# Graph layers on one core: the steps of tile 0's values and of the destination blocks set apart, and the hand-over from layer 0 to layer 1 ordered anew

## Chip, core and metric

One core of a Trainium2 chip runs the whole kernel. The metric is the device time of one execution in microseconds (us). The engines are called as in the profile: PE (TensorE), DVE (VectorE), ACT (ScalarE), POOL (GpSimd) and SP, which here only issues DMAs. Each engine works through its own instructions in the order in which the program gives them; an instruction whose input is late holds all that stand behind it.

## Reference, cut to what matters

Four graph layers run one after the other on 2708 nodes with 128 features. The change lies at the end of layer 0 and the start of layer 1.

```python
h = jnp.maximum(_layernorm(x), 0.0)
x = x + (adj.T @ h) / adj.sum(axis=0)[:, None]            # layer 0
h = jnp.maximum(_layernorm(x), 0.0)
s = h @ msg_w[:, :D].T                                     # layer 1: "sources", of row i
d = h @ msg_w[:, D:].T                                     # "destinations", of column j
messages = gelu(s[:, None, :] + d[None, :, :] + msg_b)     # only where adj is not zero
aggregated = einsum('ijd,ij->id', messages, adj)
new = gelu(concat([h, aggregated]) @ upd_w.T + upd_b) + h
x = x + layernorm(new)
# layer 2: a GRU over adj @ h;  layer 3: two heads of masked attention
```

About 0.6% of `adj` is not zero. Layer 1 is therefore done on lists of the non-zero entries.

## The kernel before

**Tiles and sets.** The nodes are cut into 22 tiles of 128 rows (the last has 20) and six groups of four tiles (the last, `LAST` = 5, has two).

**Layer 0** walks over `adj` in cuts `(c, s)`: columns of group `c`, rows of group `s`. This text calls the six cuts of one `c` a round and one cut a set. In each set DVE lists the eight largest entries of every row in each block (`list_cut`: MAX8 and FIND_INDEX8, lines 352 and 354), PE transposes the cut and multiplies it with `h0` (`work_cut`, lines 399 and 384), ACT copies the transposes out (line 406), and a DMA writes them to `adjT`. The columns of group 5 have no round of their own: their cuts (`z`) are worked in the sets of round 4 that `PARTS` names. Steps of the rows whose sums are ready are put between: norms of a finished group, its rows turned (`turn_rows`, lines 150 and 152), and its destinations.

**Three parts of a number.** Layer 1 gathers with bf16 matmuls of ones and zeros, so each f32 operand is kept as three bf16 parts. The lead is an ACT copy, the rest is src minus lead on DVE, the second part is an ACT copy of the rest, and the third part is rest minus second part on POOL. For the destinations of a group these are lines 240, 247, 248 and 249, with the scratch tile `d_rest`; for the values of a tile lines 554 to 557 (`split`) or 560 and 563 to 565 (`lead_of`, `rest_of`). A value tile also gets its columns and row ends from two POOL copies (`describe_columns`, lines 572 and 573). It all lands in `xb[t % 2]`, three parts, columns and ends side by side.

**One tile of layer 1.** `spread_ends` and `select_rows` (DVE 550 and 586) compare row numbers with the list ends and give `sel`; two DMAs move it by one row into `later`; `finish_rows` (DVE 604) subtracts. `fetch` (PE 618, ACT 619 and 623) gathers values and columns into list order through `sel`; `place` (DVE 631 to 652) picks `value` and `where`; `pass_on` (PE 668, ACT 670, one DMA) and `spread_columns` (one DMA) hand the column numbers to all partitions; `columns` (DVE 914) makes the second matrix of ones, `cols`. `find_rows` (DVE 586, tile `mine`), `put_values` (eight POOL instructions, line 897) and `put_more` (ACT 906) build the weighted matrices `put`.

**Period t of layer 1** works on four tiles at once, in six steps k. `combine(t, k)` adds sources and destinations of four blocks in PSUM (lines 971 and 975), `activate` is the Gelu (ACT 983), `gather` multiplies with `put` (PE 996). Meanwhile tile t+1 is put, tile t+2 is fetched and placed, and the rows of tile t+3 are selected.

**The start of layer 1** does not fit this pattern, since nothing has been begun. A list `run(...)` after layer 0 and a table `opening`, one row for each k of period 0, hold what has to be made up for: groups 4 and 5 are normed, turned and made into destinations here, and tiles 0 and 1 are brought forward. `manual_schedule` keeps the order of the program on every engine. PSUM tiles that are named through `bank` share two slots, so the third such tile waits until one of the two before it has been read.

Of the kernel before, what the change touches and what calls it, by code (L numbers as in the profile page):

```python
# [30 lines left out]
P = 128  # L31
N = 2708
D = 128
# [18 lines left out]
def size(t):  # L52
    return min(P, N - t * P)
# [7 lines left out]
def listed_layers(ctx: ExitStack, tc: tile.TileContext, x, adj, w, out, flag):  # L61
# [177 lines left out]
        for src, dst, q0, q1, k in state["d", g]:  # L239
            nc.scalar.copy(dst[0], src)  # L240

    def split_destinations(g):

        rest = d_rest
        for src, dst, q0, q1, k in state.pop(("d", g)):
            r = rest[0:k, q0:q1, :]
            nc.vector.tensor_tensor(r, src, dst[0], ALU.subtract)
            nc.scalar.copy(dst[1], r)
            nc.gpsimd.tensor_tensor(dst[2], r, dst[1], ALU.subtract)  # L249

# [276 lines left out]

    def last_destinations():
        destinations(LAST - 2)
        yield  # L530

    def list_last(n):
# [39 lines left out]
        nc.gpsimd.tensor_copy(x[:, :, 3 * S : 4 * S], col[:, t, :, :])  # L572
        nc.gpsimd.tensor_copy(x[:, :, C - 1], ends[:, t, :])

    def rest_tile(t):
        r = d_rest[:, 2 * t : 2 * t + 2, :].rearrange("p q d -> p (q d)")
        return r[:, 0 : NB * S].rearrange("p (b s) -> p b s", s=S)

    def describe(t, rest):
        split(*values_of(t), rest)  # L580
# [93 lines left out]
    def spread_columns(t):  # L674
# [4 lines left out]
            st["spread"].rearrange("p b e -> p (b e)"), st.pop("passed").rearrange("b e -> (b e)").partition_broadcast(P)  # L679
        )  # L680

    PARTS = {1: (0,), 2: (1, 2), 3: (3,), 4: (4, 5)}
    order = [(c, s) for c in range(LAST) for s in range(len(GROUPS))]
    mask_near(0, 0)
    for i, (c, s) in enumerate(order):
        g0, gk = GROUPS[s]
        list_cut(c, s, g0)
        if i == 0:
            state["f", 0] = factors(*state.pop(("m", -1)))
            list_cut(c, s, g0 + 1)  # L690
            state["m", 1] = moments(tiles_of(xs, *GROUPS[1]), "n4")
            list_cut(c, s, g0 + 2)
            state["f", 1] = factors(*state.pop(("m", 1)))
            list_cut(c, s, g0 + 3)
# [12 lines left out]
        if i + 1 < len(order):  # L707
            mask_near(*order[i + 1])
        if i > BEHIND and i - 1 - BEHIND + RING < len(order):
            load_cut(*order[i - 1 - BEHIND + RING])  # L710
        for z in {(LAST - 2, 3): (0,), (LAST - 2, 4): (1,), (LAST - 2, 5): (2,), (LAST - 1, 2): (3,), (LAST - 1, 3): (4, 5)}.get(
            (c, s), ()
        ):
            load_cut(LAST, z)
        if c > 0 and s == (2 if c < LAST - 1 else 1):
            turn_sums(c - 1)
        if (c, s) == (LAST - 1, LAST):
            turn_rows(LAST - 2)
            turn_sums(LAST)
        work_cut(c, s, first_steps(s) if c == 0 else next_steps(c, s))  # L720
        if c > 1 and s == 0:
            turn_rows(c - 2)
        if c > 1 and s == 1:
            destinations(c - 2)
        if c > 1 and s == (3 if c < LAST - 1 else 2):
            split_destinations(c - 2)
        if c == LAST - 1:
            if s == 1:
                ranked = rank(0, FIRST, bank("p_r"))
            if s == LAST - 1:  # L730
                pass_on(0)
            for z in PARTS.get(s, ()):
                mask_near(LAST, z)
                work_cut(LAST, z)
            if s == 1:
                nc.vector.tensor_copy(*ranked)
                spread_ends(0)
                select_rows(0)
            if s == 2:
                describe(0, rest_tile(0))  # L740
                finish_rows(0)
            if s == 3:
                for q in range(2):
                    fetch(0, q)
                place(0)
            if s == LAST - 1:
                for _ in lift(LAST):
                    pass

        if (c, s) == (1, 2):  # L750
            nc.sync.dma_start(msg_wT, w["msg_wT"])
        if (c, s) == (2, 3):
            nc.sync.dma_start(msg_b, w["msg_b"].partition_broadcast(P))
            nc.gpsimd.tensor_copy(src_self[:, 0, :], msg_wT[:, 0, :])
            nc.gpsimd.tensor_tensor(src_self[:, 1, :], msg_wT[:, 0, :], msg_wT[:, 1, :], ALU.add)

    write_one()

    add(LAST)
    measure(LAST)  # L760
    for _ in lift(LAST - 1):
        pass
    split_destinations(LAST - 2)
    turn_sums(LAST - 1)
    ending.close()
    l0.close()
# [32 lines left out]
    with (  # L799
# [116 lines left out]
        own_rows, aggs, projected = {}, {}, {}  # L916

        def project(k):

            p = projected[k] = bank("p_s") if k else mpool.tile([P, 4, D], F32, name="p_m").rearrange("p q d -> p (q d)")  # L920
            for q in range(2):
                c, mq = (2 * k + q) * P, size(2 * k + q)
                nc.tensor.matmul(
                    p[0:mq, q * 2 * D : (q + 1) * 2 * D], hT[:, c : c + mq],
                    src_self.rearrange("p c d -> p (c d)"), start=True, stop=True,
                )

        def sources(k):

            if k not in projected:  # L930
                project(k)
            pv = projected.pop(k).rearrange("p (t c d) -> p t c d", t=2, c=2)
            sb = once.tile([P, 2, 2, D], F32, name="sb")
            m = size(2 * k + 1)
            if m < P:
                nc.vector.memset(sb[:, 1, :, :], 0.0)
            bv = msg_b.unsqueeze(1).to_broadcast([P, 2, D])
            if m == P:
                bv = msg_b.unsqueeze(1).unsqueeze(1).to_broadcast([P, 2, 2, D])
                nc.vector.tensor_tensor(sb, pv, bv, ALU.add)  # L940
            else:
                for q in range(2):
                    mq = size(2 * k + q)
                    nc.vector.tensor_tensor(sb[0:mq, q, :, :], pv[0:mq, q, :, :], bv[0:mq, :, :], ALU.add)
            s3 = three.tile([P, 3, 2, D], BF16, name="s3")
            lead_of([s3[:, q, :, :] for q in range(3)], sb[:, :, 0, :])
            state["sb"] = sb
            own_rows[k] = s3, None

        def sources_rest(k):  # L950
# [135 lines left out]
        def period(t, opening):  # L1086
# [6 lines left out]
            for k in range(GB):  # L1093
# [22 lines left out]
                        project(t // 2 + 1)  # L1116
                if (t, k) in mixes:
                    mix(mixes[t, k])
                if k in ((1, 2) if begun else (4, 5)) and b:
                    fetch(t + 2, k - (1 if begun else 4))  # L1120
                if k == 1 and a:
                    lead_of(*values_of(t + 3))
                if k == 1:
# [14 lines left out]
                    check_lists()  # L1138
                if k > 0 and c and begun:
                    put_more(t + 1, k)  # L1140
                if k > 2 and not begun:
                    for q in range(2 * k - 6 + (k == 3), min(2 * k - 4, GB)):
                        put_more(t + 1, q)
                if k == (3 if begun else GB - 1) and c:
                    columns(t + 1)
                if k == 3 and t == WIDE_AT:
                    place_wide()
                if k == (3 if begun else GB - 1) and b:
                    place(t + 2)
# [27 lines left out]
        def run(*steps):  # L1177
            for step, *numbers in steps:
                step(*numbers)

        run(
            (spread_columns, 0), (spread_ends, 1), (select_rows, 1), (sources, 0), (find_rows, 0), (describe, 1, rest_tile(1)),
            (rows, 5), (sources_rest, 0), (add, 4), (measure, 4), (put_values, 0), (turn_rows, 5), (columns, 0),
            (put_more, 0, 1), (put_more, 0, 2), (finish_rows, 1),
        )
        opening = {
            0: ((put_more, 0, 3),),
            1: ((fetch_both, 1), (spread_ends, 2), (select_rows, 2), (rows, 4)),
            2: ((put_more, 0, 4), (place, 1), (find_rows, 1), (turn_rows, 4), (put_more, 0, 5)),
            3: ((describe_next, 2), (finish_rows, 2), (pass_on, 1), (spread_columns, 1), (destinations, 4), (put_values, 1)),  # L1190
            4: ((split_destinations, 4), (destinations, 5)),
            5: ((split_destinations, 5),),
        }
        for t in range(NT + 1):
            period(t, opening if t == 0 else {})
# [878 lines left out]
```

## Time and profile before

| | |
|---|---|
| median of 3 runs | 998.86 us (998.2 to 1002.5) |
| the profiled execution | 1005.51 us, of which its span is 1003.7 us |
| busy in the span | PE 918.7, DVE 793.0, ACT 532.0, POOL 444.0 us |
| mean granted TensorE clock | 0.955 |

Times inside the execution are counted from the start of its span. Layer 0 ends, and layer 1 begins, at about 200 us. A view of windows gives for each stretch the busy time of PE, of PE's weight loads, of DVE, ACT and POOL, then the granted clock and the load of the DMA engines. In a view of waits, "A <- B: total, times, longest" says that engine A sat idle until B had finished. In a timeline each row is start, duration, engine, line and operation; brackets hold the idle time before it and what ended it.

### The profile page before, as it was taken

What the parts mean: (1) busy time and instruction counts of PE and PEld (TensorE: products, weight loads), DVE (VectorE), ACT (ScalarE), POOL (GpSimd) and SP (SyncE); (2) the same over time, 40 slices, a digit from 0 to 9 for tenths busy, and PEclk for the clock granted to TensorE, in tenths of its full rate; (3) what the DMA queues carried; (4) which work ended last, traced back from release to release, by engine and by line L of the source; (5) the groups of instructions that cost most, each with busy time, mean ns of one, the idle gap of its engine ahead of it and who ended that gap; (6) DMA issues with size and microseconds to landing.
All of it is one profiled execution on the core that took longest, in us unless ns stands there. A gap on an engine that the chain in (4) does not pass through costs nothing. (4 is left out here: it accounts for less than half of the span.)

```text
span 1003.7 us, 21971 instructions
## 1 busy us (share of the span) xinstructions
PE 918.7 (92%) x7948; PEld 746.5 (74%) x7948; DVE 793.0 (79%) x2753; ACT 532.0 (53%) x1561; POOL 444.0 (44%) x524
## 2 busy tenths in 40 slices
PE   6799998964999999999999999999889999999983
PEld 3465555663999999899899644444678999999972
DVE  8999998772988898979965565666488977997793
ACT  5776665663665767656666324332321653564342
POOL 5402221354987596967975444444111300430142
PEclk9999999865999999999999899999899999999996
DMA  9899997422544443334323365764301674457000
GB/s 336 276 353 359 351 364 265 164 64 77 164 134 134 127 146 109 112 101 133 105 89 122 119 201 190 242 207 151 92 22 56 192 238 135 149 184 221 6 17 15
DMA packets 81736, 163.61 MB, mean 163 GB/s; under 512 B 9100, under 2 KB 27056, under 8 KB 81618
## 3 DMA queue, kind: packets, MB, share of 16 engines
q1 hardware_dynamic: 62518, 129.98, 40.5%
q10 hardware_dynamic: 19100, 32.13, 8.7%
q8 instruction: 64, 1.05, 0.4%
q14 instruction: 54, 0.44, 0.1%
HBM read 115.47 MB, written 30.87 MB: 146 GB/s over the span
## 5 line engine op out<-in xcount | busy, mean ns | idle before, releaser
L897 POOL TENSOR_SCALAR put<-count,line,value 128x128 f32<-128x128 f32 x176 | 195.3, 1122 | 18.7 <-DVE value L652 18.0
L1283 PE MATMUL att<-hv,wt 128*128 128x129 f32 x1672 | 196.2, 278 | 7.4 <-DVE wt L1253 6.0
L1283 PEld LDWEIGHTS att<-hv,wt 128*128 128x128 f32 x1672 | 192.5, 194 | 10.5 <-DVE wt L1253 8.5
L975 PE MATMUL p_m<-d,cols 128*128 128x128 bf16 (+1 forms) x1452 | 163.9, 222 | 16.8 <-POOL d L249 9.1
L971 PE MATMUL p_m<-s,sel 128*128 128x128 bf16 x1452 | 163.5, 222 | 6.6 <-ACT g L983 6.2
L1253 DVE SCALAR_TENSOR_TENSOR wt<-row,lift,mask 128x1024 f32<-128x1024 f32 (+1 forms) x132 | 138.8, 1082 | 23.3 <-PE att L1283 23.2
L121 POOL TENSOR_TENSOR n_r<-n_r,minus_half 128x4 f32<-128x4 f32 (+1 forms) x28 | 40.4, 1441 | 243.3 <-DVE n_r L120 241.6
L996 PE MATMUL agg<-put,g 128*128 128x128 f32 (+1 forms) x968 | 128.0, 286 | 0.0
L996 PEld LDWEIGHTS agg<-put,g 128*128 128x128 f32 x968 | 117.3, 198 | 2.5 <-issue 0.4
L384 PE MATMUL sums<-a,h 128*128 128x512 f32 x220 | 116.7, 627 | 1.6 <-ACT h L137 1.6
L971 PEld LDWEIGHTS <-sel 128*128 128x128 bf16 x1452 | 104.5, 99 | 17.1 <-issue 16.5
L983 ACT ACTIVATE g<-p_m 128x512 f32<-128x512 f32 x132 | 72.8, 553 | 76.0 <-PE agg L996 48.3
L975 PEld LDWEIGHTS <-cols 128*128 128x128 bf16 (+1 forms) x1452 | 102.7, 99 | 11.6 <-issue 5.5
L1444 PE MATMUL p_agg<-a,hs 128*128 128x512 f32 (+2 forms) x264 | 108.1, 551 | 2.6 <-DMA a<-adjT 2.5
L399 PEld LDWEIGHTS p_T<-ident,a 128*128 128x128 f32 (+1 forms) x440 | 55.7, 145 | 63.3 <-issue 41.2
L906 ACT ACTIVATE put<-mine,value 128x128 f32<-128x128 bf16 x308 | 100.8, 393 | 0.0
L354 DVE FIND_INDEX8 col<-val,a 128x8 uint16<-128x128 f32 x327 | 89.3, 284 | 0.0
L1444 PEld LDWEIGHTS p_agg<-a,hs 128*128 128x128 f32 (+1 forms) x264 | 47.3, 192 | 50.0 <-issue 45.7
L406 ACT ACTIVATE aT<-p_T 128x512 f32<-128x512 f32 (+2 forms) x132 | 71.0, 540 | 23.6 <-PE p_T L399 21.2
L399 PE MATMUL p_T<-ident,a 128*128 128x128 f32 (+1 forms) x440 | 71.3, 283 | 12.9 <-ACT aT L406 6.7
L1406 ACT ACTIVATE hs<-hs 128x1354 f32<-128x1354 f32 (+1 forms) x44 | 58.5, 1329 | 39.8 <-DMA hs<-in_adj 39.4
L352 DVE MAX8 val<-a 128x8 f32<-128x128 f32 x327 | 77.2, 276 | 0.0
(292 smaller groups left out, 1522.5 us busy)
## 6 DMA issues: line engine op xcount, KB each, us to landing
hs<-in_adj SPq DMA_DIRECT2D x42, 677.0 KB
adjT<-aT ACTq DMA_DIRECT2D x50, 512.0 KB
a<-adjT SPq DMA_DIRECT2D x20, 1280.0 KB
a<-in_adj SPq DMA_DIRECT2D x24, 1024.0 KB
spread<-passed SPq DMA_DIRECT2D x22, 704.0 KB
later<-sel SPq DMA_DIRECT2D x22, 616.0 KB
cols_a<-in_adj SPq DMA_DIRECT2D x11, 320.0 KB
row<-own_d ACTq DMA_DIRECT2D x10, 256.0 KB
```

What stands on the lines that cost most here:

```text
L352: nc.vector.max(val[0:m, n, b, :], v)
L354: nc.vector.max_index(col[0:m, n, b, :], val[0:m, n, b, :], v)
L384: nc.tensor.matmul(accs[c][:, 0:w], h0[0:m, n, :], a[0:m, n - g0, t0 * P - lo : t0 * P - lo + w], start=(n == 0), stop=(n == NT - 1),)
L399: nc.tensor.transpose(p[0:k, i * iw + q * P : i * iw + q * P + m], a[0:m, q, e : e + k], ident[0:m, 0:m])
L897: nc.gpsimd.tensor_scalar(st["put", 0][:, b, :], count, st["line"][:, b : b + 1], st["value"][:, b : b + 1], ALU.is_equal, ALU.mult,)
L906: nc.scalar.activation(st["put", 1][:, b - HP, :], st["mine"][:, b - HP, :], AF.Identity, scale=st["value"][:, b : b + 1])
L971: nc.tensor.matmul(p[:, b - b0, :], st["sel"][:, b, :], s3[:, q, t % 2, :], start=(q == 0), stop=False)
L975: nc.tensor.matmul(p[:, b - b0, :], st["cols"][0:kb, b, :], d3[0:kb, b, q, :], start=False, stop=(q == 2))
L996: nc.tensor.matmul(agg, g[:, b - 4 * k, :], put, start=(b == 0), stop=False)
L1253: nc.vector.scalar_tensor_tensor(wt[:, 0:n], row[:, k, c : c + n], lift[:, j, k : k + 1], mask[:, j, c : c + n], op0=ALU.max, op1=ALU.mult,)
L1283: nc.tensor.matmul(banks[s // 3][:, s % 3, :], wt[:, q * P : (q + 1) * P], hv[:, j, k, :], start=(v < 2 and s // 3 not in touched), stop=( ...
L1444: nc.tensor.matmul(pa[:, 0:n], h[0:k, j, :], a[0:k, j - j0, 0:n], start=(j == 0), stop=(j == NT - 1))
```

## The change

It sets steps apart that stood together, and orders the end of layer 0 and the start of layer 1 anew.

- **Destinations in layer 0.** `split_destinations` becomes `take_lead` (the DVE subtraction, in set 2 of a round) and `split_rest` (the ACT copy and the POOL subtraction, in set 3).
- **Values of tile 0.** `describe(0)` in set 2 of round 4 becomes `lead_of` (ACT, set 1), `less_lead` (DVE, set 2) and `pass_rest` (ACT and POOL, set 3). The rest has a tile of its own instead of a part of `d_rest`.
- **Placing of tile 0.** `place(0)` moves from set 3 to set 4, and `pass_on(0)` from set 4 into set 5, where the projection for the sources of tiles 0 and 1 (`project(0)`) now follows it.
- **End of layer 0.** Tile 1's values, the bias of the sources and the last norm of group 5 come ahead of the last turned sums.
- **Run and opening.** Group 5's destinations and group 4's norm come into the run; group 4's destinations come ahead of `combine(0, 2)`; `fetch_both(2)` comes ahead of `combine(0, 4)`; the puts of tile 0 stand later, and those of tile 1 have other places.

```diff
-    def split_destinations(g):
+    def take_lead(g, rest=None):
+        state["r", g] = []
         for src, dst, q0, q1, k in state.pop(("d", g)):
-            r = rest[0:k, q0:q1, :]
+            r = (d_rest if rest is None else rest)[0:k, q0:q1, :]
             nc.vector.tensor_tensor(r, src, dst[0], ALU.subtract)
+            state["r", g].append((r, dst))
+    def split_rest(g):
+        for r, dst in state.pop(("r", g)):
             nc.scalar.copy(dst[1], r)
             nc.gpsimd.tensor_tensor(dst[2], r, dst[1], ALU.subtract)
...
     def last_destinations():
         destinations(LAST - 2)
+        pass_on(0)
+        project(0)
         yield
...
+    def less_lead(t):
+        dst, src = values_of(t)
+        rest = state["x", t] = opener.tile([P, NB, S], F32, name="hot")
+        nc.vector.tensor_tensor(rest, src, dst[0], ALU.subtract)
+    def pass_rest(t):
+        dst, rest = values_of(t)[0], state.pop(("x", t))
+        nc.scalar.copy(dst[1], rest)
+        nc.gpsimd.tensor_tensor(dst[2], rest, dst[1], ALU.subtract)
+        describe_columns(t)
...
         work_cut(c, s, first_steps(s) if c == 0 else next_steps(c, s))
+        if c > 1 and s == 3:
+            split_rest(c - 2)
+        if (c, s) == (LAST - 1, 3):
+            pass_rest(0)
...
-        if c > 1 and s == (3 if c < LAST - 1 else 2):
-            split_destinations(c - 2)
+        if c > 1 and s == 2:
+            take_lead(c - 2)
...
-            if s == LAST - 1:
-                pass_on(0)
...
                 select_rows(0)
+                lead_of(*values_of(0))
             if s == 2:
-                describe(0, rest_tile(0))
+                less_lead(0)
                 finish_rows(0)
             if s == 3:
                 for q in range(2):
                     fetch(0, q)
+            if s == LAST - 1:
                 place(0)
...
     write_one()
+    lead_of(*values_of(1))
+    take_lead(LAST - 2, pool.tile([P, 4, D], F32, bufs=1, name="part_x"))
     add(LAST)
     measure(LAST)
+    less_lead(1)
+    add_bias(0, d_rest.rearrange("p (t c) d -> p t c d", t=2))
+    spread_ends(1)
+    split_rest(LAST - 2)
+    rows(LAST)
+    pass_rest(1)
     for _ in lift(LAST - 1):
         pass
-    split_destinations(LAST - 2)
     turn_sums(LAST - 1)
...
-                if k in ((1, 2) if begun else (4, 5)) and b:
-                    fetch(t + 2, k - (1 if begun else 4))
+                if k in (1, 2) and b and begun:
+                    fetch(t + 2, k - 1)
...
-                if k > 2 and not begun:
-                    for q in range(2 * k - 6 + (k == 3), min(2 * k - 4, GB)):
+                if not begun:
+                    for q in {4: (1, 2), 5: (3, 4, 5)}.get(k, ()):
                         put_more(t + 1, q)
...
         run(
-            (spread_columns, 0), (spread_ends, 1), (select_rows, 1), (sources, 0), (find_rows, 0), (describe, 1, rest_tile(1)),
-            (rows, 5), (sources_rest, 0), (add, 4), (measure, 4), (put_values, 0), (turn_rows, 5), (columns, 0),
-            (put_more, 0, 1), (put_more, 0, 2), (finish_rows, 1),
+            (spread_columns, 0), (select_rows, 1), (take_sources, 0), (turn_rows, 5), (sources_rest, 0), (add, 4), (measure, 4),
+            (destinations, 5), (take_pair, 5), (split_rest, 5), (columns, 0), (rows, 4), (put_values, 0), (finish_rows, 1),
+            (spread_ends, 2), (find_rows, 0),
         )
         opening = {
-            0: ((put_more, 0, 3),),
-            1: ((fetch_both, 1), (spread_ends, 2), (select_rows, 2), (rows, 4)),
-            2: ((put_more, 0, 4), (place, 1), (find_rows, 1), (turn_rows, 4), (put_more, 0, 5)),
-            3: ((describe_next, 2), (finish_rows, 2), (pass_on, 1), (spread_columns, 1), (destinations, 4), (put_values, 1)),
-            4: ((split_destinations, 4), (destinations, 5)),
-            5: ((split_destinations, 5),),
+            1: ((turn_rows, 4), (fetch_both, 1), (select_rows, 2), (put_more, 0, 1)),
+            2: ((destinations, 4), (put_more, 0, 2), (put_more, 0, 3), (take_lead, 4), (place, 1)),
+            3: (
+                (split_rest, 4), (pass_on, 1), (spread_columns, 1), (describe_next, 2), (finish_rows, 2),
+                (put_more, 0, 4), (put_more, 0, 5),
+            ),
+            4: ((fetch_both, 2), (find_rows, 1), (put_values, 1)),
+            5: ((place, 2),),
         }
```

`project` and `add_bias` are the two halves of the old `sources`, brought out of layer 1's block; `take_sources` is the rest of it (the lead of the sources, on ACT). For tiles 0 and 1 the projection's PSUM tile is now one of layer 0's sums tiles, and the biased sources lie in `d_rest` instead of a tile of their own. `take_pair(5)` is `take_lead` with a scratch tile of layer 1, and `find_rows(0)` and `find_rows(1)` stand later than before. In periods after the first, the program is the same.

More of the change, by code (lines that the diff above doesn't have):

```diff
@@ L240, in destinations @@
             nc.scalar.copy(dst[0], src)
-    def split_destinations(g):
-        rest = d_rest
+    def take_lead(g, rest=None):
+        state["r", g] = []
         for src, dst, q0, q1, k in state.pop(("d", g)):
-            r = rest[0:k, q0:q1, :]
+            r = (d_rest if rest is None else rest)[0:k, q0:q1, :]
             nc.vector.tensor_tensor(r, src, dst[0], ALU.subtract)
+            state["r", g].append((r, dst))
+    def split_rest(g):
+        for r, dst in state.pop(("r", g)):
             nc.scalar.copy(dst[1], r)
@@ L573, in describe_columns @@
         nc.gpsimd.tensor_copy(x[:, :, C - 1], ends[:, t, :])
-    def rest_tile(t):
-        r = d_rest[:, 2 * t : 2 * t + 2, :].rearrange("p q d -> p (q d)")
-        return r[:, 0 : NB * S].rearrange("p (b s) -> p b s", s=S)
+    def less_lead(t):
[7 more added lines that the diff above has]
+        describe_columns(t)
     def describe(t, rest):
@@ L680, in spread_columns, with project, add_bias @@
         )
+    own_rows, projected = {}, {}
+    def project(k):
+        p = projected[k] = bank("p_s") if k else sump.tile([P, CH], F32, name="sums")
+        for q in range(2):
+            c, mq = (2 * k + q) * P, size(2 * k + q)
+            nc.tensor.matmul(
+                p[0:mq, q * 2 * D : (q + 1) * 2 * D], hT[:, c : c + mq],
+                src_self.rearrange("p c d -> p (c d)"), start=True, stop=True,
+            )
+    def add_bias(k, sb):
+        state["sb"] = sb
+        pv = projected.pop(k).rearrange("p (t c d) -> p t c d", t=2, c=2)
+        m = size(2 * k + 1)
+        if m < P:
+            nc.vector.memset(sb[:, 1, :, :], 0.0)
+            bv = msg_b.unsqueeze(1).to_broadcast([P, 2, D])
+            for q in range(2):
+                mq = size(2 * k + q)
+                nc.vector.tensor_tensor(sb[0:mq, q, :, :], pv[0:mq, q, :, :], bv[0:mq, :, :], ALU.add)
+        else:
+            bv = msg_b.unsqueeze(1).unsqueeze(1).to_broadcast([P, 2, 2, D])
+            nc.vector.tensor_tensor(sb, pv, bv, ALU.add)
     PARTS = {1: (0,), 2: (1, 2), 3: (3,), 4: (4, 5)}
@@ L744, in listed_layers @@
                     fetch(0, q)
+            if s == LAST - 1:
                 place(0)
-            if s == LAST - 1:
                 for _ in lift(LAST):
@@ L914, in columns, with take_sources @@
             nc.vector.tensor_scalar(st["cols"], st.pop("spread"), part, None, ALU.is_equal)
[L916 to L926, printed above, removed]
+        aggs = {}
         def sources(k):
+            sb = once.tile([P, 2, 2, D], F32, name="sb")
             if k not in projected:
                 project(k)
[L932 to L944, printed above, removed]
+            add_bias(k, sb)
+            take_sources(k)
+        def take_sources(k):
             s3 = three.tile([P, 3, 2, D], BF16, name="s3")
-            lead_of([s3[:, q, :, :] for q in range(3)], sb[:, :, 0, :])
-            state["sb"] = sb
+            lead_of([s3[:, q, :, :] for q in range(3)], state["sb"][:, :, 0, :])
             own_rows[k] = s3, None
@@ L1147, in period @@
                     place_wide()
+                if k == 3 and b and begun:
+                    place(t + 2)
                 if k == (3 if begun else GB - 1) and b:
-                    place(t + 2)
                     find_rows(t + 2)
@@ L1179, in run, with take_pair @@
                 step(*numbers)
-        run(
-            (spread_columns, 0), (spread_ends, 1), (select_rows, 1), (sources, 0), (find_rows, 0), (describe, 1, rest_tile(1)),
-            (rows, 5), (sources_rest, 0), (add, 4), (measure, 4), (put_values, 0), (turn_rows, 5), (columns, 0),
-            (put_more, 0, 1), (put_more, 0, 2), (finish_rows, 1),
+        def take_pair(g):
+            take_lead(g, once.tile([P, 2, D], F32, name="s_r"))
+        run(
+            (spread_columns, 0), (select_rows, 1), (take_sources, 0), (turn_rows, 5), (sources_rest, 0), (add, 4), (measure, 4),
+            (destinations, 5), (take_pair, 5), (split_rest, 5), (columns, 0), (rows, 4), (put_values, 0), (finish_rows, 1),
+            (spread_ends, 2), (find_rows, 0),
         )
         opening = {
-            0: ((put_more, 0, 3),),
-            1: ((fetch_both, 1), (spread_ends, 2), (select_rows, 2), (rows, 4)),
-            2: ((put_more, 0, 4), (place, 1), (find_rows, 1), (turn_rows, 4), (put_more, 0, 5)),
-            3: ((describe_next, 2), (finish_rows, 2), (pass_on, 1), (spread_columns, 1), (destinations, 4), (put_values, 1)),
-            4: ((split_destinations, 4), (destinations, 5)),
-            5: ((split_destinations, 5),),
+            1: ((turn_rows, 4), (fetch_both, 1), (select_rows, 2), (put_more, 0, 1)),
[6 more added lines that the diff above has]
+            5: ((place, 2),),
         }
```

## Prediction

> **What bounds the kernel now.** I read the windows first, in stretches of 10 us around the end of layer 0 (start:end, length, then busy PE, weight loads, DVE, ACT, POOL, granted clock, DMA share, GB/s):
>
> ```profile
> 160.00:170.00 10.00, 7.21 (x42) 4.88 (x40) 10.00 (x62) 3.85 (x16) 0.23 (x1) 1.00 0.83 264
> 170.00:180.00 10.00, 8.38 (x37) 5.58 (x38) 5.22 (x23) 7.34 (x26) 4.69 (x8) 0.83 0.77 259
> 190.00:200.00 10.00, 9.67 (x31) 5.06 (x31) 4.42 (x23) 4.03 (x21) 0.70 (x1) 0.65 0.46 155
> 200.00:210.00 10.00, 4.15 (x14) 2.52 (x13) 7.70 (x23) 5.23 (x11) 3.41 (x5) 0.50 0.28 85
> 220.00:230.00 10.00, 5.53 (x59) 4.79 (x58) 7.09 (x11) 6.17 (x19) 5.82 (x7) 0.86 0.23 74
> 230.00:240.00 10.00, 2.96 (x34) 2.80 (x34) 1.34 (x3) 1.68 (x7) 6.05 (x8) 0.50 0.40 119
> 240.00:250.00 10.00, 6.78 (x59) 5.99 (x58) 1.91 (x6) 3.79 (x14) 1.73 (x5) 0.61 0.01 2
> 260.00:270.00 10.00, 10.00 (x147) 9.59 (x145) 8.36 (x28) 5.52 (x18) 10.00 (x13) 1.00 0.38 125
> ```
>
> In layer 0 DVE binds until 170 (it is busy without a gap there, as in nearly every 5 us stretch from 20 on). From 260 PE binds (10.00 of 10.00). Between the two nothing binds for long: from 170 to 180 DVE has 5.22 us of work, and from 200 to 250 PE has 27.6 of 50. A microsecond taken out of that stretch moves the whole PE-bound layer 1 forward, and layers 2 and 3 hang on it, so I count it in full. Next the waits and the timeline, for who waits:
>
> ```profile
> DVE d_r L555 <- ACT xb L554: 4.8, 1, 4.8
> ACT d L248 <- DVE d_r L247: 9.8, 3, 5.6
> PE p_m L975 <- POOL d L249: 9.1, 2, 8.1
> DVE d_r L247 <- POOL d L249: 7.2, 1, 7.2
> PE p_h L150 <- ACT hs L137: 3.9, 1, 3.9
> ...
> 170.36 0.62 ACT L248 CAST d<-d_r 128x512 bf16<-128x512 f32 x1 [5.57 <-DVE d_r L247]
> 175.11 0.34 DVE L555 TENSOR_TENSOR d_r<-val,xb 128x176 f32<-128x176 f32 x1 [4.78 <-ACT xb L554]
> 226.94 1.63 DVE L586 TENSOR_TENSOR sel<-count_h,ends 128x2816 bf16<-128x2816 bf16 x1
> 227.06 1.65 POOL L573 COPY xb<-ends 128x22 bf16<-128x22 bf16 x1
> 228.63 6.30 POOL L897 TENSOR_SCALAR put<-count,line,value 128x128 f32<-128x128 f32 x8
> 236.10 0.27 PE L975 MATMUL p_m<-d,cols 128*128 128x128 bf16 x1 [8.10 <-POOL d L249]
> 241.93 0.27 POOL L573 COPY xb<-ends 128x22 bf16<-128x22 bf16 x1
> ```
>
> Two places stand out. At 165 to 175 ACT waits 5.57 us for the DVE subtraction of the destinations; when it has caught up, DVE waits 4.78 us for ACT's lead of tile 0's values. In period 0 the third part of group 4's destinations stands on POOL behind the eight puts of tile 1, and `combine(0, 4)` waits 8.10 us for it. Group 5's parts follow (DVE waits 7.2; PE waits 2.24 and 0.99 more).
>
> **Part 1, the steps set apart in round 4.** Nothing is added; each step only finds its input done. DVE ends the lists of set 2 at 169.65 as before, and `take_lead` ends at 170.3. Then come `less_lead` 0.34, its lead long made, and `finish_rows(0)` 1.62, so the lists of set 3 begin at 172.3 instead of 176.90: **DVE −4.6**. From 176.9 to 191.5 DVE was full, so its lists end at 186.9 instead of 191.5. PE and ACT lose their 4.41 us gap, and about 0.9 us of slow clock after it, so DVE sets the gain. DMA is loaded (0.83 of the share): the transposes that are now written early wait for buffers, perhaps 1 us on ACT, inside the 5.3 that ACT gains. In rounds 2 and 3 the same split takes away the other 4.2 us of ACT waits; I cost that at nothing, since DVE is full there. If DVE were not, it could gain those 4.2. `place(0)`, 2.9 us of DVE, stands a set later, in the same queue.
>
> **Part 2, the hand-over.** PE reaches the turned rows of group 3 at 185.6 (190.93 − 5.3) and ends the `destinations(3)` behind them at 188.8 (2.05 us up to them, 1.1 for eight matmuls). Now `pass_on(0)` stands there and needs a `bank` slot: one holds group 5's sums, the other these destinations. That wait is new. The destinations' slot is free when ACT has copied the lead (0.58, to 189.8) and DVE has subtracted (0.69, to 190.5); PE waits 1.7. Behind it on PE are `project(0)` (four matmuls, 1.92 in the row at half clock, 1.1 at full), two sets of transposes (about 1.3) and the last products (4.08 at half clock): PE ends at about 197.6 instead of 200.05. On SP the two DMAs of tile 0's columns are issued some 2 us later than 189.10 and 191.17; `cols` needs them at 204, which covers it, and a cover that failed would cost at most those 2 us.
>
> DVE in the meantime does what used to stand behind the end of layer 0: group 5's add and moments (2.5), tile 1's rest (0.34), the bias (0.69) and five small factors (1.3). After the end there were 11.65 us from PE's last product (200.05) to `cols` (211.72). Now it is `sel` 1.62, the sources' rest 0.41, group 4's add 2.0 and moments 1.95, group 5's pair 0.48, `cols` 0.95, which is 7.4; ACT's lift, Gelu table (1.28) and copies let DVE wait for a few tenths only. `cols` is done at 197.6 + 7.4 = 205.0: **−6.8**, part 1 included.
>
> Here a rule is weighed. The row: the clock fell to 0.5 at 193 with PE busy in every 2 us around it, and the last four products took 4.08, where two at full clock take 1.02. The Trainium skill, "TensorE: Matmul & The Clock Gate", Part 1, lays the half clock to idle windows of 3.4 us; by that alone, without gaps, the products would take 2.04. But its Part 4 on transposes says that these do not count as activity in the same way, and this stretch is mostly transposes. By Part 1 alone PE ends at 195.6 and the gain is 1 to 2 us more. I follow the row and keep the half clock.
>
> **Part 3, period 0**, counted from the end of `cols` (C; before 211.72, after 205.0). Before, `combine(1, 0)` began at C + 35.7. After, in PE's order: `combine(0, 0)` to C + 2.6 (24 matmuls at half clock), `turn_rows(4)` after group 4's norm (C + 2.9, four scalings 1.65) to C + 3.8, `fetch_both(1)` 0.9, `combine(0, 1)` 2.2, `project(1)` 1.1, `destinations(4)` 1.1, `combine(0, 2)` 1.35: C + 10.7. `pass_on(1)` needs `where`: ACT's lead at C + 9.9, DVE's `take_lead(4)` 0.69, then `place(1)`: C + 12.2, a wait of 1.6. `combine(0, 3)` and two gathers (1.35 + 2.0): C + 15.9. Then the wait that takes the old one's place: **`fetch_both(2)` now stands ahead of `combine(0, 4)`** and needs `xb` of tile 2. ACT copies tile 1's sources, Gelus and scales until C + 16.2, then group 4's second part to C + 16.8; POOL follows with line 249 and with lines 557, 572 and 573.
>
> The second rule speaks against the change. Line 573 takes 0.27 alone and 1.65 beside `sel` (rows above). The Trainium skill, "GPSIMD Engine Reference", 1. Specifications, says that POOL shares its SBUF interfaces with DVE and contends with DVE instructions that have two SBUF inputs; `finish_rows(2)` (1.62) and `find_rows(1)` (1.08) are such and run just then. Uncontended the four take 1.15 + 0.54 + 0.36 + 0.27 = 2.3; contended 1.46 + 1.45 + 0.36 + 1.65 = 4.9, by the slowest rows. I take 3.7: `xb` at C + 20.5, PE waits 4.6. The puts of tile 1 come behind it on POOL and hold nothing until period 1.
>
> Then `fetch_both(2)` 0.9, `combine(0, 4)` and `(0, 5)` 2.0, two gathers 2.0, and some 1.8 of half clock after the gap: `combine(1, 0)` at C + 27.3. That is **−8.4**. `cols` of tile 1 (C + 26), the puts of tile 0 on POOL (C + 9) and ACT (C + 20) are in time.
>
> **Sum.** 6.8 + 8.4 = 15.2, less 0.7 for what queues on ACT, which is nearly full from C + 10 to C + 30: **14.5 us**. The profiled execution had a span of 1003.7 and a time of 1005.51, so it would go to about 991. It stands 0.7% above the median of 998.86; I take the gain off the median: 984.4. From both ends: with the slowest POOL rows and a full slow clock in period 0, about 10; with the clock at full in the hand-over and POOL uncontended, about 18.
>
> **The rivals.** (a) *The stall is only moved.* PE now meets the serial chain group 4's norm, turn, destinations, `take_lead`, `place(1)`, sources, `xb` of tile 2 ahead of its combines, where it used to have four combines in hand. If each of the three heads (`turn_rows(4)`, `pass_on(1)`, `fetch_both(2)`) waits 2.5 us longer than I count, 7 us are left: 992. For it: DVE and ACT are 70 and 60% busy there already. Against: the 8 us of puts no longer stand in that chain. (b) *Only period 0 gains*, the tail of layer 0 being held by loads: DMA share was 0.83, and the chain of loads could keep set 3 late. Then about 9 us: 990. Against: set 3's cut was issued at 137.0, long before. (c) *Slower:* `pass_on(0)` on PE waits not for the destinations' slot but for group 5's sums, read by `add(5)` only later, and everything behind it, the last products and with them the release of layer 0's memory for `sel`, shifts by the same. By my count that costs 1.4 more; it decides only where the hand-over and the chain of (a) lose 20 us together: 1004. (d) *It doesn't do what it says:* the parts are cut, but the queue order leaves ACT waiting as before; then within 2 us.
>
> **How the numbers follow.** A difference under 0.5% (5 us) can hardly be told from none here. My forecast (gain 10 to 19) has 0.68; (a) and (b) together 0.20; (d) and small gains 0.05; (c) 0.07. Range 979 to 993.5: from the forecast's best end with a microsecond of spread to the far end of (a).
>
> **What would show it.** ACT's wait at line 248 and DVE's at 555 in round 4 gone; the lists of round 4 ending near 187; the first `cols` near 205; no 8 us wait of line 975 for POOL, but one of 3 to 6 us ahead of line 618 in period 0; the first matmul of period 1 near 232 instead of 247; and after that a PE as full as before. I am wrong if PE still idles over 12 us between `cols` and period 1, if the lists end at 191 as before, or if layer 1 from there to its end takes longer than before.

## The result and the profile after

| | before | after |
|---|---|---|
| median of 20 runs each | 1000.55 us (996.82 to 1006.33) | 995.65 us (992.33 to 999.11) |
| ratio, 95% interval | | 0.995 [0.9936, 0.9964] |
| profiled execution: time, span, granted clock | 1005.51, 1003.7, 0.955 | 992.33, 990.5, 0.966 |

The change takes 4.9 us off the median. 14.5 us were forecast. The two profiled executions are 13.2 us of span apart, which is nearly the forecast; but before's profile is one of its late executions and after's is the earliest of its 20. Two more profiles of before and one of after, below, show what of the 13.2 belongs to the change.

The windows after, in the columns of the prediction (start:end, length, busy PE, weight loads, DVE, ACT, POOL, granted clock, DMA share, GB/s):

```profile
160.00:170.00 10.00, 9.33 (x57) 6.52 (x55) 10.00 (x62) 4.19 (x17) 1.17 (x4) 1.00 0.83 257
170.00:180.00 10.00, 6.25 (x28) 3.91 (x29) 10.00 (x55) 6.50 (x24) 2.49 (x6) 0.83 0.82 293
180.00:190.00 10.00, 6.98 (x46) 4.54 (x46) 6.86 (x32) 3.97 (x13) 5.00 (x14) 0.83 0.15 55
190.00:200.00 10.00, 8.33 (x53) 6.00 (x51) 2.17 (x10) 6.50 (x31) 0.63 (x2) 1.00 0.33 122
200.00:210.00 10.00, 7.37 (x19) 2.92 (x18) 7.93 (x29) 5.70 (x15) 3.89 (x6) 0.52 0.60 184
220.00:230.00 10.00, 6.86 (x70) 6.49 (x68) 6.27 (x13) 5.83 (x17) 4.74 (x6) 0.83 0.19 61
230.00:240.00 10.00, 5.56 (x70) 5.45 (x71) 8.77 (x12) 4.93 (x18) 9.75 (x9) 0.83 0.58 191
240.00:250.00 10.00, 10.00 (x157) 9.98 (x156) 6.95 (x17) 7.81 (x27) 10.00 (x11) 1.00 0.43 144
```

Two things are to be seen. DVE no longer idles from 170 to 180 (10.00 where it had 5.22), and PE is full from 240 to 250 (10.00 where it had 6.78). But PE has wider holes than before: it is busy for 6.25 us from 170 to 180 (8.38 before) and for 6.98 from 180 to 190 (10.00 before). From 190 to 200 DVE stands nearly empty (2.17). The waits of that stretch (engine, line, releaser; total, times, longest) say for what:

```profile
DVE part_x L247 <- ACT d L240: 9.5, 1, 9.5
PE y L632 <- POOL xb L580: 9.2, 2, 5.2
...
ACT aT L411 <- DMA z<-in_adj: 3.9, 1, 3.9
...
ACT aT L411 <- DMA a<-in_adj: 2.5, 1, 2.5
...
PE p_w L682 <- DVE where L665: 2.4, 1, 2.4
...
ACT aT L411 <- DMA adjT<-aT: 1.9, 1, 1.9
...
PE p_w L682 <- DVE part_x L247: 1.4, 1, 1.4
```

ACT's old wait of 5.57 us for DVE is gone, and ACT now waits 3.9 + 2.5 + 1.9 = 8.3 us for landings of DMAs. Before, such waits came to 1.6 us in the same stretch:

```profile
ACT aT L406 <- DMA a<-in_adj: 1.0, 1, 1.0
...
ACT aT L406 <- DMA adjT<-aT: 0.6, 1, 0.6
```

PE's `fetch` (line 632) waits twice for POOL's `xb`: one wait of 5.2 was forecast (4.6), the other was not. DVE's 9.5 us is the end of the same story: its lists are done, and it waits for the destinations of group 3, which PE brings late. The timeline, in order of time (start, duration, engine, line, what, and in brackets the idle time before it):

```profile
166.42 0.59 ACT L411 ACTIVATE aT<-p_T 20x512 f32<-20x512 f32 x1 [2.52 <-DMA a<-in_adj]
...
171.54 0.59 ACT L411 ACTIVATE aT<-p_T 20x512 f32<-20x512 f32 x1 [3.87 <-DMA z<-in_adj]
...
174.13 0.60 ACT L411 ACTIVATE aT<-p_T 128x512 f32<-128x512 f32 x1 [1.92 <-DMA adjT<-aT]
...
183.02 0.79 PE L632 MATMUL y<-xb,sel 128*128 128x37 bf16 x22 [3.97 <-POOL xb L580]
...
193.85 0.66 PE L150 MATMUL p_h<-ident,hs 128*128 128x128 f32 x4
...
197.66 0.69 DVE L247 TENSOR_TENSOR part_x<-p_d,d 128x512 f32<-128x512 f32 x1 [9.51 <-ACT d L240]
...
200.16 3.88 PE L389 MATMUL sums<-a,h 128*128 128x512 f32 x4
...
211.49 0.93 DVE L965 TENSOR_SCALAR cols<-spread,part 128x2816 bf16<-128x2816 bf16 x1
...
232.74 1.65 POOL L580 COPY xb<-ends 128x22 bf16<-128x22 bf16 x1
234.44 0.84 PE L632 MATMUL y<-xb,sel 128*128 128x37 bf16 x22 [5.22 <-POOL xb L580]
...
240.54 0.33 PE L1004 MATMUL p_m<-s,sel 128*128 128x128 bf16 x3
```

The first `cols` is done at 212.42, where before had 211.72 and the forecast 205.0. So at the start of period 0 nothing is won in this profile. From there to the first matmul of period 1 (240.54) it is 28.1 us where it was 35.7, and PE idles for 7.6 of them where it idled for 13.9: period 0 is what the change gains.

### The profile page after: what moved, and what is told of

It reads as the page before. It is cut to its first block, busy times and chain, and to the rows that moved or that the text cites. A ratio compares the mean times of both kernels' runs of the same rounds, so it can differ in the third digit from the quotient of the medians.

```text
span 990.5 us, 21970 instructions
## 1 busy us (share of the span) xinstructions
PE 912.2 (92%) x7948; PEld 742.2 (75%) x7948; DVE 797.3 (80%) x2753; ACT 532.2 (54%) x1561; POOL 445.1 (45%) x524
## 5 line engine op out<-in xcount | busy, mean ns | idle before, releaser
L948 POOL TENSOR_SCALAR put<-count,line,value 128x128 f32<-128x128 f32 x176 | 199.6, 1145 | 11.2 <-DVE value L666 10.1
L1322 PEld LDWEIGHTS att<-hv,wt 128*128 128x128 f32 x1672 | 192.4, 194 | 10.5 <-DVE wt L1292 8.5
L1029 PE MATMUL agg<-put,g 128*128 128x128 f32 (+1 forms) x968 | 124.9, 281 | 0.0
L1029 PEld LDWEIGHTS agg<-put,g 128*128 128x128 f32 x968 | 114.5, 194 | 2.4 <-issue 0.2
```

The source lines that it names most:

```text
L948: nc.gpsimd.tensor_scalar(st["put", 0][:, b, :], count, st["line"][:, b : b + 1], st["value"][:, b : b + 1], ALU.is_equal, ALU.mult,)
L1029: nc.tensor.matmul(agg, g[:, b - 4 * k, :], put, start=(b == 0), stop=False)
L1322: nc.tensor.matmul(banks[s // 3][:, s % 3, :], wt[:, q * P : (q + 1) * P], hv[:, j, k, :], start=(v < 2 and s // 3 not in touched), stop=( ...
```

## The experiments

Marks used below are the end of the lists of round 4, the start of `turn_rows(3)` on PE, the end of the first `cols`, and the close of tile 0 (the last `agg` matmul of its sums, 244.7 in the profile after). Medians of before in the three series were 999.82, 1000.29 and 1000.06 us.

**The two halves, each alone.** `layer0_only` has the layer-0 side on the kernel before: steps cut apart, `place(0)` and `pass_on(0)` later. End of layer 0, run and opening are before's. `start_only` is the opposite, the changed kernel with the old order inside layer 0 (`place(0)` and `pass_on(0)` stand a set sooner again, too).

```diff
 # layer0_only, on the kernel before
+        if c > 1 and s == 3:
+            split_rest(c - 2)
+        if (c, s) == (LAST - 1, 3):
+            pass_rest(0)
...
-        if c > 1 and s == (3 if c < LAST - 1 else 2):
-            split_destinations(c - 2)
+        if c > 1 and s == 2:
+            take_lead(c - 2)
 # start_only, on the kernel after
-        if c > 1 and s == 2:
+        if c > 1 and s == (3 if c < LAST - 1 else 2):
             take_lead(c - 2)
+            split_rest(c - 2)
...
             if s == 2:
+                lead_of(*values_of(0))
                 less_lead(0)
+                pass_rest(0)
```

> The kernel before with only the layer-0 side of the change: destinations split over sets 2 and 3, tile 0's values over sets 1 to 3, place(0) in set 4, pass_on(0) in set 5; end of layer 0, run and opening as before. Theory 1 (the tail of layer 0 gained nothing: ACT's wait for DVE became waits for the DMAs that write adjT, and fetch(0) now waits for tile 0's xb on POOL): the lists of round 4 end near 188 instead of 191.7, but the first cols come at 211 to 215 instead of 211.7; time 0 to 0.4% above the kernel before. Theory 2 (part 1 of the prediction was right, and its gain was lost later): cols near 207, time 0.4% below.

> The change with its layer-0 side undone: destinations and tile 0's values split at one place as before, place(0) in set 3, pass_on(0) in set 4; end of layer 0 (with project(0) in set 5), run and opening as changed. Theory 1: keeps the whole gain of the change or more, 0.5 to 0.9% below the kernel before; period 1 begins some 28 us after the first cols, as in the changed kernel. Theory 2: it lacks the 4.6 us of part 1 and is slower than the changed kernel by 0.4%.

Measured: `layer0_only` 1000.46 us, ratio 1.0 [0.9983, 1.0016]. `start_only` 993.31 us, ratio 0.9929 [0.99, 0.9957]. The layer-0 side alone is worth nothing (its first `cols` are done at 211.56), and the change is no better with it than without. Waits of `layer0_only`, 160 to 250:

```profile
ACT aT L419 <- DMA z<-in_adj: 4.1, 1, 4.1
PE y L643 <- DVE val L365: 4.0, 1, 4.0
...
ACT aT L419 <- DMA a<-in_adj: 2.5, 1, 2.5
...
ACT aT L419 <- DMA adjT<-aT: 1.7, 1, 1.7
```

The same three waits for landings (8.3 us) come with the cut steps, and so does a wait of 4.0 us at the fetch of tile 0 (line 643 here, at 183.05). In `start_only` one landing is left for ACT, and the fetch of tile 0 waits for nothing (the row of line 631 is that of tile 2 in period 0, the row of `cols` that of tile 2, at 244.9):

```profile
PE y L631 <- POOL xb L579: 6.9, 1, 6.9
...
DVE cols L964 <- DMA spread<-passed: 1.3, 1, 1.3
ACT aT L411 <- DMA adjT<-aT: 0.8, 1, 0.8
```

Lists of round 4 end at 188.2 in `layer0_only` and at 190.5 in `start_only` (191.65 before), so DVE does come sooner with the cut. `turn_rows(3)` on PE goes the other way: 193.87 against 190.94 (190.93 before). What follows the lists is taken from PE's chain. Two five-microsecond windows around it, before and then after:

```profile
180.00:185.00 5.00, 5.00 (x52) 3.83 (x51) 4.97 (x31) 4.14 (x16) 3.99 (x12) 1.00 0.52 196
185.00:190.00 5.00, 5.00 (x33) 3.45 (x31) 4.79 (x23) 4.54 (x19) 1.21 (x4) 1.00 0.48 188
```

```profile
180.00:185.00 5.00, 1.98 (x27) 1.84 (x27) 3.92 (x22) 0.71 (x4) 4.75 (x14) 0.83 0.14 52
185.00:190.00 5.00, 5.00 (x20) 2.70 (x19) 2.94 (x11) 3.26 (x10) 0.25 (x1) 0.83 0.16 57
```

Before, PE was as full as DVE here (5.00 of 5.00 twice). After, it loses 3 us from 180 to 185, and the clock falls for a while.

**One wait each taken away from the changed kernel.** `fetch0_late` fetches tile 0 a set later, behind POOL's last step. `loads_early` issues the load of cut (4, 4) one set sooner. `aT6` tests the thought behind the "1 us on ACT" of the prediction: it gives the transposes that are to be written (`aT`) a sixth buffer, and takes the room from the tiles of the pool `marked`.

```diff
 # fetch0_late
-            if s == 3:
+            if s == LAST - 1:
                 for q in range(2):
                     fetch(0, q)
-            if s == LAST - 1:
                 place(0)
 # loads_early
-        if i > BEHIND and i - 1 - BEHIND + RING < len(order):
+        if i > BEHIND and i - 1 - BEHIND + RING < len(order) and (c, s) != (LAST - 1, 2):
...
+        if (c, s) == (LAST - 1, 1):
+            load_cut(LAST - 1, 4)
 # aT6
-    marked = l0.enter_context(tc.tile_pool(name="l0n", bufs=8))
-    turned = l0.enter_context(tc.tile_pool(name="l0t", bufs=5))
+    marked = l0.enter_context(tc.tile_pool(name="l0n", bufs=4))
+    turned = l0.enter_context(tc.tile_pool(name="l0t", bufs=6))
```

> The changed kernel with fetch(0) in set 4 of round 4, just ahead of place(0), instead of set 3. Theory 1: PE's wait of 4.0 us for xb at 179 to 183 goes, with the half clock behind it; the first cols come at 207 to 209 instead of 212.4, and the time falls 0.3 to 0.5% below the changed kernel, to about 0.991 of the kernel before. Rival (DMA alone holds the tail): ACT is late anyway, cols stay within 1 us of 212.4, ratio 0.995.

> The changed kernel with the load of cut (4, 4) issued one set earlier, ahead of select_rows(0)'s two DMAs on SP instead of behind them, so that 1 MB leaves the crowded stretch from 163 to 176. Theory 1: ACT's waits for DMA between 164 and 175 (8.3 us in three) fall to 4 us or less, the turned rows of group 3 come 2 to 4 us earlier on PE, the first cols about 2 us earlier; ratio to the kernel before 0.992 to 0.994. Rival (the wait is on the queue of the adjT writes itself, or on fetch(0) alone): ACT's waits stay at 7 us or more, ratio 0.995.

> The changed kernel with six instead of five aT tiles (room made by four instead of eight near tiles). If ACT's waits in 164 to 175 are for an aT tile that a DMA has yet to write out: one tile more takes 2 us or more off the 8.3, and the turned rows of group 3 come 1 to 3 us earlier than 194.2. If they are for the landing of loads: the waits stay at 8 us, and so does everything else; ratio 0.995.

Measured: `fetch0_late` 991.88 us, 0.9935 [0.9914, 0.9957]; `loads_early` 993.72, 0.9933 [0.9913, 0.9954]; `aT6` 995.42, 0.9961 [0.9931, 0.999]. The first two are each some 1.6 us better than the change (0.995), though their intervals touch its own. Waits of `fetch0_late`:

```profile
PE y L632 <- POOL xb L580: 5.2, 1, 5.2
ACT aT L411 <- DMA z<-in_adj: 3.8, 1, 3.8
...
ACT aT L411 <- DMA a<-in_adj: 2.5, 1, 2.5
ACT aT L411 <- DMA adjT<-aT: 2.3, 1, 2.3
```

The wait of `fetch(0)` is gone (one wait of line 632 is left, that of period 0), and ACT's waits stay. `turn_rows(3)` comes at 190.03, the first `cols` at 210.0. Waits of `loads_early`, then of `aT6`:

```profile
PE y L632 <- POOL xb L580: 5.2, 1, 5.2
ACT aT L411 <- DMA z<-in_adj: 5.0, 1, 5.0
```

```profile
ACT aT L411 <- DMA z<-in_adj: 3.8, 1, 3.8
...
ACT aT L411 <- DMA later<-sel: 2.5, 1, 2.5
...
ACT junk L270 <- DMA adjT<-aT: 1.3, 1, 1.3
```

With the load issued sooner ACT waits 5.0 us for landings instead of 8.3. With another buffer it waits 7.6. So a lack of buffers is not the main cause: the prediction had the right place and the wrong reason. `loads_early` came to the ratio that was expected of it, but not to the signs: its turned rows (193.18) and its first `cols` (211.75) are each only 0.7 us sooner than in the profile after, the close of tile 0 is the same (244.7), and its fetch still waits 3.4 us at 181.25. So it is not shown that its 1.6 us are won at the start.

What ties ACT to the loads stands in the semaphore records of the traces. (A semaphore is a counter on which an instruction can wait.) Every DMA reports its landing on one of eight semaphores, which loads on SP and writes of `adjT` on ACT use in turn, 49 or 50 DMAs each. Ahead of the writes in question stands a wait of ACT for the semaphore of that write, and it ends 0.02 us after the last landing of the DMA that had the semaphore before. The copy that the rows name stands behind that issue in ACT's queue. In the profile after, the write issued at 165.94 has the semaphore of the `later` issued at 161.13, whose last landing is at 165.87 (the row names `a`). The write at 171.13 has that of the `z` issued at 164.27, which landed at 171.05. Only the third wait is for a buffer: the copy at 174.13 waits for the write of 165.94, which landed at 174.05. In `aT6` the copy goes at 172.91 instead, and the next write then waits for the same kind of landing, until 174.45, because it has the semaphore of that earlier write. An edit that moves a load also shifts whose semaphore a write gets: in `loads_early` the write at 163.32 has one that has been free since 159.97. No run changes the semaphores alone.

**All together, and the other order in period 0.** `start_fetch2` is `start_only` with `fetch_both(2)` moved behind `combine(0, 4)`, for the wait of 5 to 7 us ahead of the fetch of tile 2. `all_three` is the change with that move, `fetch0_late` and `loads_early`. `start_loads` is `start_only` with the load of `loads_early`. `three_aT6` is `all_three` with the sixth buffer.

```diff
 # start_fetch2, all_three, three_aT6
-            4: ((fetch_both, 2), (find_rows, 1), (put_values, 1)),
-            5: ((place, 2),),
+            4: ((find_rows, 1), (put_values, 1)),
+            5: ((fetch_both, 2), (place, 2)),
 # start_loads, on start_only
+        if (c, s) == (LAST - 1, 1):
+            load_cut(LAST - 1, 4)
```

> The kernel start_only (hand-over and opening of the change, layer 0 as before) with fetch_both(2) behind combine(0, 4), in row 5 of the opening ahead of place(2). If the wait for tile 2's xb is what is left in period 0 (6.9 us in start_only): combine(0, 4) fills some 2.5 us of it, but cols of tile 1, behind place(2) on DVE, then ends period 0, so tile 0's close comes 1 to 2 us earlier than 241.2; ratio 0.990 to 0.993. If POOL's order sets the end anyway: close at 241 as before, ratio 0.993.

> The changed kernel with all three edits: fetch(0) in set 4, cut (4, 4) loaded one set earlier, fetch_both(2) behind combine(0, 4). Theory 1: the gains add up in part: first cols 208 to 210, tile 0's close 239 to 242, ratio 0.989 to 0.992. Rival (each only moves the wait): close at 242 to 243 as with fetch(0) alone, ratio 0.9935.

> The kernel start_only with cut (4, 4) loaded one set earlier. The layer-0 side is as before, where DMA waits were only 0.8 us in all, so the earlier load should bring nothing: first cols 209 to 210, tile 0's close 241, ratio 0.993. If DMA did hold this tail too: 1 to 2 us earlier, ratio 0.991 to 0.992.

> The kernel all_three with six aT tiles: the best version that the theories so far point to. If aT tiles were a limit: cols 206 to 208, tile 1's close 253 or earlier, ratio 0.987 to 0.990. If not: the same as all_three within 0.2%, 0.989 to 0.993.

Measured:

| kernel | median us | ratio [95%] | first `cols` | close of tile 0 | close of tile 1 |
|---|---|---|---|---|---|
| start_only | 993.31 | 0.9929 [0.99, 0.9957] | 209.6 | 241.2 | 254.8 |
| start_fetch2 | 994.28 | 0.9942 [0.993, 0.9955] | 208.9 | 239.2 | 255.2 |
| start_loads | 991.45 | 0.9904 [0.9872, 0.9936] | 209.2 | 241.1 | 254.6 |
| all_three | 991.16 | 0.9908 [0.9887, 0.9928] | 208.8 | 239.1 | 255.0 |
| three_aT6 | 992.47 | 0.9914 [0.9882, 0.9946] | 208.7 | 239.9 | 255.9 |

`start_fetch2` is a miss. It closes tile 0 2 us sooner, and tile 1 then takes 16.0 us instead of 13.6: the wait of period 0 is paid back in period 1. Moving this fetch gains nothing, then, and the gain of `all_three` is put down to the other two edits. In the same series as the unchanged copy of the changed kernel its interval stands apart from that one's (0.9908 [0.9887, 0.9928] against 0.9964 [0.9949, 0.9979]). So the two waits that the layer-0 side brought cost some 4 to 6 us together. The close of tile 1, in one or two profiles each, says the same: 258.3 and 259.7 for the changed kernel, 258.2 for `loads_early`, 256.2 for `fetch0_late`, 255.0 for `all_three`, 254.8 for `start_only`. By these the fetch's wait is the larger part. `three_aT6` shows that the sixth buffer brings nothing here either.

`start_loads` reaches the same time with layer 0 in its old order: even freed of the two waits, the cut steps bring nothing that the old order lacks. But nothing was expected of its earlier load (0.993), and 0.9904 came. The intervals of `start_only` and `start_loads` overlap, and their marks at the start are only 0.1 to 0.4 us apart, so part of what the earlier load gives may not lie in these waits at all. The waits of `start_loads` name one landing, 0.9 us ahead of the `cols` of tile 2:

```profile
PE y L631 <- POOL xb L579: 5.2, 1, 5.2
...
DVE cols L966 <- DMA spread<-passed: 0.9, 1, 0.9
```

`start_loads` and `all_three`, some 9 us below before, have the lowest ratios of the versions that ran.

**The unchanged kernels once more.** One profile cannot tell how much of its stretch is chance, so both kernels were profiled again, with no edit.

> The kernel before once more, for a second profile of it and for the noise of the comparison. Theory 1 (the first stretch is the same in every execution, and the two profiled executions of before and of the change differ by luck behind it, 13.2 us of span against 4.9 us of medians): row of tile 0's close near 252.9 again, span 995 to 1001, ratio 1.000 within 0.2%. Rival (the start itself varies by several us from execution to execution): the close moves by over 2 us.

> The changed kernel once more. Theory 1: tile 0's close near 244.7 again (8.2 us ahead of before), span 990 to 996, ratio 0.992 to 0.996. Rival (8 us at the start are not kept): span 995 or more although the close is at 244.7, with the loss between tile 1 and layer 2.

> A third profile of the kernel before. Theory (which half of the 3.4 us clock windows the start falls in moves the start by some 5 us, with the same program): where the stretch from 193 to 217 is mostly at half clock, cols come near 211.7 and tile 0's close near 252.9, as in the first profile; where it is mostly at full clock, near 208.5 and 248.2, as in the second. Rival (the clock has no part in it): the close does not go with the clock.

`before_again` had a median of 999.83 us (0.9984 [0.9959, 1.0009]), `after_again` 996.72 (0.9964 [0.9949, 0.9979]); `before_third` is one run of 1001.2.

| profile | first `cols` | close of tile 0 | between | half clock, 190 us to that close | span |
|---|---|---|---|---|---|
| before | 211.7 | 252.9 | 41.2 | 44.4 | 1003.7 |
| before_again | 208.5 | 248.2 | 39.7 | 20.5 | 998.3 |
| before_third | 207.7 | 249.1 | 41.4 | 30.7 | 999.4 |
| after | 212.4 | 244.7 | 32.3 | 23.9 | 990.5 |
| after_again | 213.5 | 246.1 | 32.6 | 23.9 | 998.2 |

The windows of `before_again`, to be set against the clock of 0.65 and 0.50 that the prediction read in the same two stretches:

```profile
190.00:200.00 10.00, 8.99 (x48) 5.64 (x46) 5.49 (x21) 6.36 (x28) 1.32 (x2) 1.00 0.59 196
200.00:210.00 10.00, 2.92 (x21) 1.91 (x20) 9.16 (x29) 7.12 (x19) 5.08 (x7) 0.74 0.28 85
```

The same program ran the tail of layer 0 at full clock this time and was done with its first `cols` 3.2 us sooner. The last four products of layer 0, before and then in `before_again`, show what the clock does:

```profile
195.97 4.08 PE L384 MATMUL sums<-a,h 128*128 128x512 f32 x4
```

```profile
195.98 2.18 PE L384 MATMUL sums<-a,h 128*128 128x512 f32 x4
```

From the turned rows of group 3 (190.9, 192.1 and 191.3) to the end of `cols` the three profiles of before take 20.8, 16.4 and 16.4 us, at a mean granted clock of 0.55, 0.89 and 0.86. So the first profile, on which the prediction rested, was late in this stretch by 4.4 us, with the same 40 matmuls in it and the clock mostly at half. Mean close of tile 0 is 250.1 in three profiles of before and 245.4 in two of after: 4.7 us, near the 4.9 of the medians. That they are so near is partly luck, for the three of before are themselves up to 4.7 us apart. What comes behind that close takes 750 to 751 us in the three of before and 745.8 and 752.1 in the two of after, so the other 5 us in the spans' difference of 13.2 belong to no edit.

## Why the prediction was right and wrong

**Right: period 0.** From `cols` to the start of period 1 the prediction said 27.3 us; 28.1 came. The waits that it put at the heads were near: `pass_on(1)` 1.6 forecast, 2.35 measured; `fetch_both(2)` 4.6 forecast, 5.22 measured. POOL's copy of `xb` did take its slow 1.65. The four POOL instructions ahead of that fetch took 5.4 us, though, where 3.7 had been taken and 4.9 by the slowest rows; the wait came near its count partly by luck, because PE reached it 0.9 us later than counted. Over all five profiles the stretch from `cols` to the close of tile 0 went from a mean of 40.8 to 32.5 us: −8.3, where −8.4 was the forecast (up to the first matmul of period 1). `pass_on(0)` waited 1.40 for its bank (1.7 forecast), so rival (c) stayed as small as it was priced. The columns' DMAs were covered, as forecast: the first `cols` waits for no landing.

**Wrong: the way to the first `cols`.** The forecast was −6.8 us there; the means are 209.3 before and 213.0 after, +3.7. That is 10.5 us. Less the 0.7 that was set aside for ACT, and with 0.1 in period 0, it is the whole gap between 14.5 and 4.7. By its steps:

- "PE and ACT lose their 4.41 us gap … so DVE sets the gain" is the step that failed. DVE did gain (lists done at 188.15; 191.65 before, 186.9 forecast). But before, PE was full as well from 180 to 190, so PE had to come sooner too, and it came later: turned rows of group 3 at 193.85 instead of the forecast 185.6. DVE then waited 9.5 us. The 8.2 us that PE lost against the forecast are, in the profile after, of three parts. PE stood ready for the fetch of tile 0 at 179.05, where 5.3 us ahead of before would have been 176.3: 2.8 us. It waited there for 3.97 us. From the fetch (183.02) to the turned rows it took 10.8 us where before took 9.35, with the granted clock at 0.83 instead of 1.00 from 180 to 190: 1.5 us. The fetch before:

```profile
181.58 0.71 PE L618 MATMUL y<-xb,sel 128*128 128x37 bf16 x22
```

- "perhaps 1 us on ACT, inside the 5.3 that ACT gains" is the mis-sized term. ACT waited 8.3 us for landings, 6.7 more than before, which is more than the 5.57 taken away. Once freed of DVE, ACT ran ahead into writes whose semaphores still belonged to loads on their way. PE in turn waited 3.5 us for ACT's copies, and so had only 2.5 of its 5.3 us at the fetch.
- `pass_rest(0)` was costed at nothing, as a step that finds its input done. One set later in POOL's queue it stands behind the sum of squares of the new set (lines 275 to 281, which start at 178.15 and end at 180.9) and a step of the destinations, and the fetch of tile 0 behind it waited 3.97 us. Who reads the result of the last of the cut steps was not asked. `fetch0_late` shows that wait removed: turned rows at 190.03, `cols` 2.4 us sooner.
- The base was a late execution. The forecast took 6.8 off 211.7; two more profiles of before have 208.5 and 207.7, so 2.4 us of it, against the mean, were not in a usual execution. From the turned rows to `cols` the forecast was 19.4 us, and both profiles of after have 18.6. That is less than the 20.8 of the profile that was read, but more than the 16.4 of the two others: against these, the new order of the hand-over itself takes 2.2 us longer.

**The rule weighed.** The half clock was kept, against what the Trainium skill, "TensorE: Matmul & The Clock Gate", Part 1, would have given. In the profile after it came again: it began at 200.4, with no gap of PE over 1.4 us from 195 to 200 (3.60 busy of 5), and the last four products took 3.88 us. But in `after_again` and in both other profiles of before these products took 2.18 us, at full clock. So neither choice was right as a constant; the products take either time. The reason given for the choice fits only the 3.4 us ahead of the fall, where transposes take 2.4 us; of PE's 9.67 us from 190 to 200 they take 3.3. The half-clock times of the table (20.5, 23.9, 30.7, 44.4 us) are 6, 7, 9 and 13 times 3.41 us, which agrees with the windows of 3.4 us that the page states.

**The rivals.** (b), only period 0 gains, is what happened, though not by a late load of set 3 as it was told: the cause is the landings for which ACT's writes waited, and the fetch on PE. Its own price was 9 us and the change gave 4.9, because the hand-over lost microseconds besides. (a) and (d) did not come: the waits at the heads were near the count, and the old waits of ACT and DVE were gone.

Still open: what the earlier load gains in `loads_early` and `start_loads`, and how exactly the cost of 4 to 6 us divides between the two waits.

## What to carry to other kernels

A wait that is taken out of a stretch where DMA is loaded can turn into waits for landings. Price it between nothing and somewhat more than the wait removed: here 5.57 us went and 6.7 came. When a copy seems to wait for a load that it doesn't read, look at what its engine issues just ahead of it, and on which semaphore. When a helper is cut into steps that stand further apart, cost the step that ends last: who reads it, and what is ahead of it now in each queue. Where the clock falls in a stretch, read a second profile before a microsecond is counted from the first, because one execution is only one of many.

## What the runs showed of the hardware

The same program's place in time at the end of layer 0 moves by 4 us between executions (first `cols` at 207.7, 208.5 and 211.7). From the turned rows to these `cols` the latest of the three has a mean granted clock of 0.55 and takes 20.8 us, the other two 0.86 and 0.89 and 16.4 us; the same four products take 4.08 us in the one and 2.18 in the others. In all 14 traces every stretch of half clock is a whole multiple of 3.41 us long, apart from the one that the end of the execution cuts off. What decides whether the clock falls in a given execution, no run here shows.

An issue of a DMA can itself be what an engine waits at: ACT's write at 171.13 was held until 171.07, 0.02 us after a load on another queue, whose semaphore it had, landed at 171.05.
